# A Hadamard transform of weights in two exact single-pass halves instead of one full-precision product

## The chip, the cores and the metric

The kernel runs on one core of one Trainium2 chip. The metric is the time of one execution on the device in microseconds (us). A core has five engines that run their own instruction queues in order: PE (TensorE, matrix products), DVE (VectorE), ACT (ScalarE), POOL (GpSimd) and SP (SyncE, which only issues DMAs here). "PEld" is PE's loading of the stationary operand, which overlaps with its products.

## The reference, cut to what matters

The input `x` is 8 sequences of 512 tokens of 512 features, all float32. Each token is layer-normalized. One branch is linear attention (three projections, `elu + 1`, a running sum over tokens, an output projection), the other a gated feed-forward layer whose weights stand behind Walsh-Hadamard transforms (`fwht`); their product is added to `x`:

```
x = fwht(xn * SU_ug) / SCALE
x_up   = x @ W_up.T   * (Wscale_ug[:INTER] * SCALE)
x_gate = x @ W_gate.T * (Wscale_ug[INTER:] * SCALE)
x = fwht(silu(x_gate) * x_up * SU_dp) / SCALE
g = silu(x @ W_down.T * (Wscale_dp * SCALE))
out = x0 + attention(xn) * g
```

A transform of a product's input is the same as a transform of its weights, so the kernel transforms the three weight matrices (512 x 2048 each) once, on the chip, and then multiplies by those. A transform over 512 features splits into a 128-point one across the partitions, which is a product with the 128x128 matrix of plus and minus ones (`had`), and two rounds of butterflies (sum and difference) between the four blocks of 128. Over 2048 features there are four such rounds.

## The kernel before, in words

**Work and stages.** The eight sequences go in four pairs (p = 0 to 3). For a pair, all large products (q, k, v, out, gate, up, down) are done by a fast scheme that makes a 2x2 block product from seven factor products (places P1 to P7, in the order P1, P2, P7, P3, P4, P5, P6 of a tile `[128, 2, 7, 128]`); the weights' seven factors are encoded by four DVE instructions per block (`encode_weights`, lines 310 to 315). In the first pair the weights are also prepared: read, transformed, encoded and written to DRAM, from which the later pairs stream them ready-made. So everything that the change touches lies in the first pair, before about 360 us of the profiled span.

**The gate and up weights** (`folded_w`, line 926) are 16 blocks (gate 0 to 7, up 0 to 7). For each there are three steps: `butterflies` (four DVE instructions of 512 elements per partition, lines 937 to 940, into a fresh tile of the pool `t8`), `fold` (two matmuls with `had`, line 946, each followed by two ACT scalings of 256 columns by the signs `SU_ug`, line 952, from PSUM back into the weights' tile), and `encode`. The first product of the block's group waits for the scalings and the encoded places.

**The down weights** are four blocks of 16 tiles (o = 0 to 3): `butterflies_down` makes scale and four rounds on DVE (lines 979 and 984) in the buffer `rd`, then `fold_down` (line 993) does four matmuls with `had` (line 998), each with four ACT scalings of 128 columns (line 1004), and the block goes to DRAM (`wd_f`, line 1010). `chain_down` strings the four blocks together.

**Order.** The program is traced in an order set by an agenda: `at(n, fn)` puts a step n places ahead, one place being about one factor product, and `advance` runs them (lines 430 to 443). A list scheduler then orders each engine's queue by priority and readiness; the matmuls of the folds are held in the order of the program (`keep_in_program_order`). What comes out is a fixed queue per engine, and an engine waits at the head of its queue. PSUM banks of the folds are the tag `t`, which has two buffers, so that a fold's matmul also waits until the scalings of the fold two before it have read their bank. The groups' banks are `px` (3 buffers), `py` (1) and `pz` (2); DVE and ACT read them out (lines 465 to 476).

**Other work named later.** POOL encodes the attention's context `co` (`encode_tokens`, lines 303 to 307), the output weights `w_o` (lines 312 to 315) and the hidden activations `ho` (lines 800 to 802: products of gate and up; then lines 304 to 307). ACT makes `neg_k` and `neg_q` (lines 710 and 711) for `elu`, and DVE takes those up at line 712.

Of the kernel before, what the change touches and what calls it, by code (L numbers as in the profile page):

```python
# [7 lines left out]

F32 = mybir.dt.float32
AF = mybir.ActivationFunctionType  # L10
ALU = mybir.AluOpType
PSUM = bass.MemoryType.PSUM
# [5 lines left out]
P1, P2, P7, P3, P4, P5, P6 = range(7)  # L18
# [3 lines left out]
def kernel(  # L22
# [27 lines left out]
    nc = tc.nc  # L50
    P = 128
# [4 lines left out]
    NF = FF // P  # L56
# [6 lines left out]
    const = ctx.enter_context(tc.tile_pool(name="const", bufs=1))  # L63
# [4 lines left out]
    t8 = ctx.enter_context(tc.tile_pool(name="t8", bufs=6))  # L68
# [5 lines left out]
    @contextmanager  # L74
    def background(behind=150):

        at = tc.cur_priority
        tc.cur_priority = at + behind
        yield
        tc.cur_priority = at  # L80
# [20 lines left out]

    cols_sb = const.tile([P, cols.shape[1]], F32, tag="cols", name="cols_sb")
    offs = {}
    at = 0
# [9 lines left out]

    bo_r = const.tile([P, D], F32, tag="bo_r", name="bo_r")
    ident = const.tile([P, P], F32, tag="ident", name="ident")
    had = const.tile([P, P], F32, tag="had", name="had")
    ones = const.tile([P, 1], F32, tag="ones", name="ones")
    su_ug = const.tile([P, KD], F32, tag="su_ug", name="su_ug")
    su_dp = const.tile([P, NF], F32, tag="su_dp", name="su_dp")  # L120
# [13 lines left out]
    def layernorm(b, xt, parts=1):  # L134
        n = NT // parts
        for i in range(0, NT, n):
# [6 lines left out]
            nc.vector.tensor_scalar(rstd, mv[:, :, 1], EPS, None, ALU.add)  # L143
            nc.scalar.activation(rstd, rstd, AF.Sqrt)
            nc.vector.reciprocal(rstd, rstd)
# [6 lines left out]
    def first_layernorms(xs):  # L152
# [8 lines left out]
        def pinned(ins):  # L161
            tc.keep_in_program_order(ins)

        for i in range(2 * NT + 1):
            if i < 2 * NT:
# [4 lines left out]
                pinned(nc.vector.tensor_scalar(r, mv[:, i, 1:2], EPS, None, ALU.add))  # L170
                nc.scalar.activation(r, r, AF.Sqrt)
            if i:
# [10 lines left out]
    def normalized(b):  # L183
# [246 lines left out]
    def at(place, fn):  # L430
        agenda.append((now[0] + place, now[1], fn))
        now[1] += 1
# [17 lines left out]
    def group(name, ws, rhs, dst, then, bias=(None, None), time=1.7):  # L450
# [14 lines left out]
        def snapshot(what, i):  # L465
# [5 lines left out]
            else:  # L471
                nc.scalar.activation(s, p, AF.Identity, bias=b)
            return s
# [218 lines left out]
    def attention(p, xo, co, get_w):  # L692
        def project(m, g, then):
# [4 lines left out]
            def whole(px):  # L698
                nc.scalar.activation(r[:, 0, 1], px, AF.Identity, bias=b[0])
                then(r)  # L700
# [219 lines left out]
    def butterfly(eng, dst, src, h):  # L920
# [2 lines left out]
        eng.tensor_tensor(d[:, :, 0], s[:, :, 0], s[:, :, 1], ALU.add)  # L923
        eng.tensor_tensor(d[:, :, 1], s[:, :, 0], s[:, :, 1], ALU.subtract)

    def folded_w(name, src, f, room=None):

        w = raw_w(f"{name}_{f}", src, 0, 2, 1, f * P, NG * P, room)
        places = (slice(P1, P7 + 1, 2), slice(P2, P4 + 1, 3))
        rs = []  # L930

        def butterflies():
            t = t8.tile([P, 2, 2, 2, 2, P], F32, tag="t", name=f"r_{name}_{f}")
            r2, r = t[:, 0], t[:, 1]
            rs.append(r)
            a, b = (w[:, :, place, :] for place in places)
            nc.vector.tensor_tensor(r2[:, 0], a, b, ALU.add)
            nc.vector.tensor_tensor(r2[:, 1], a, b, ALU.subtract)
            nc.vector.tensor_tensor(r[:, :, 0], r2[:, :, 0], r2[:, :, 1], ALU.add)
            nc.vector.tensor_tensor(r[:, :, 1], r2[:, :, 0], r2[:, :, 1], ALU.subtract)  # L940

        def fold():
            for b in range(2):
                p = ps.tile([P, 2, 2, P], F32, tag="t", name=f"pw_{name}_{f}_{b}")
                tc.keep_in_program_order(
                    nc.tensor.matmul(
                        p.rearrange("p j a e -> p (j a e)"), had,
                        rs[0][:, b].rearrange("p j a e -> p (j a e)"), start=True, stop=True,
                    )
                )  # L950
                for j in range(2):
                    nc.scalar.activation(
                        w[:, j, places[b], :], p[:, j], AF.Copy, scale=su_ug[:, 2 * b + j : 2 * b + j + 1]
                    )
        def encode():
            encode_weights(nc.vector, w)
            folded[name, f] = w
            if f >= NU:
                with background():
                    inner_w(name, f - NU, folded[name, f - NU], w)  # L960

        return w, [(5, butterflies), (7, fold), (9, encode)]

    folded = {}
    wd_f = dram.tile([FF, D], F32, tag="wd_f", name="wd_f")
# [3 lines left out]
    def load_down(o):  # L969
        at(14, lambda: loaded.append(o))  # L970
        nc.sync.dma_start(rs[:, o % 2], wdown_t[:, o * P : (o + 1) * P].rearrange("(c p) e -> p c e", p=P))
# [18 lines left out]
                later(1.2, half, i, dst, src, h)  # L990
        later(0.0, then)

    def fold_down(o, a, then):

        r = rs[:, o % 2]
        p = ps.tile([P, 4, P], F32, tag="t", name=f"pwd_{o}_{a}")
        tc.keep_in_program_order(
            nc.tensor.matmul(
                p.rearrange("p c e -> p (c e)"), had,
                r[:, 4 * a : 4 * a + 4].rearrange("p c e -> p (c e)"), start=True, stop=True,  # L1000
            )
        )
        for c in range(4):
            nc.scalar.activation(
                r[:, 4 * a + c], p[:, c], AF.Copy, scale=su_dp[:, 4 * a + c : 4 * a + c + 1]
            )
        if a + 1 < NF // 4:
            at(2, lambda: fold_down(o, a + 1, then))
            return
        nc.sync.dma_start(wd_f[:, o * P : (o + 1) * P].rearrange("(c p) e -> p c e", p=P), r)  # L1010
        then()
# [49 lines left out]
    def weights_ahead(u):  # L1061

        def begin(m, src, f):
            t = t8.tile([P, 2, 7, P], F32, tag="t", name=f"w_{m}_{f}")
            _, steps = folded_w(m, src, f, t)
            place = 10
            for _, step in steps:
                at(place, step)
                place += 7

        at_ = 2
        for m, src in (("gate", wgate_t), ("up", wup_t)):
            for f in (u, u + NU):
                at(at_, lambda m=m, src=src, f=f: begin(m, src, f))
                at_ += 12
# [64 lines left out]
    src = ident  # L1140
    for i in range(7):
        dst = had if i % 2 == 0 else had2
        s = src.rearrange("p (a t h) -> p a t h", t=2, h=1 << i)
# [3 lines left out]
        src = dst  # L1147
# [14 lines left out]
    rs = rd[:, : 3 * NF * P].rearrange("p (i c e) -> p i c e", i=3, e=P)  # L1162
# [8 lines left out]
    def chain_down(o):  # L1171
        if o not in loaded:
            at(2, lambda: chain_down(o))
            return

        def folded_block():
            if o + 2 < KD:
                at(8, lambda: load_down(o + 2))
            if o + 1 == KD:
                at(8, first_half_down)  # L1180

        def then():
            at(10, lambda: fold_down(o, 0, folded_block))
            if o + 1 < KD:
                at(4, lambda: chain_down(o + 1))

        butterflies_down(o, then)
# [116 lines left out]
```

## Time and profile before

| what | value |
|---|---|
| median of 3 runs | 1555.47 us (1553.84 to 1557.9) |
| span of the profiled execution, first to last instruction | 1552.4 us |
| what the median has beyond that span | 3.1 us |
| PE idle inside the span (span less busy) | 28.6 us |

The profile gives only the span of its own execution; its whole time is taken to be the span and the 3.1 us around it.

The same engine times by stretch, from the table of windows (busy us of each engine):

| stretch, us | PE | DVE | ACT | POOL |
|---|---|---|---|---|
| 0 to 69 | 60.3 of 69 | 60.9 | 30.3 | 6.9 |
| 69 to 138 | 63.4 of 69 | 64.9 | 34.5 | 33.2 |
| 138 to 430 | 283.5 of 292 | 215.7 | 81.4 | 71.9 |
| 430 to 1552 | 1116.6 of 1122 | 660.8 | 272.7 | 324.7 |

To read such tables: an engine that is busy all the time need not be the one that sets the end, since work can be queued on it that nobody needs yet. The chain of waits says which engine the end was waiting for at each moment. "Busy" of DVE and POOL also counts the time in which an instruction has started but stands still. PE had its full granted clock (0.998 on average).

### The profile page before, as it was taken

The page shows a single profiled execution, that of the slowest core. Times are in us where ns is not written, and L with a number is a line of the kernel's source. Part 1 is how long each engine was busy: PE and PEld are TensorE (multiplying, and loading weights), DVE is VectorE, ACT ScalarE, POOL GpSimd, SP SyncE. Part 2 cuts the span into 40 slices and gives each one's busy share as a digit, 9 for nine tenths or more (in the row PEclk, how much of TensorE's full clock was granted, in tenths as well). Part 3 has the DMA queues.
Part 4 walks back from the last instruction along what each step waited for, and adds up shares of the span by engine and source line. Part 5 has one row for each costly group of instructions (what it writes and reads, how often), then busy time and mean ns, then how long its engine had stood idle before and what let it go on. Part 6 is the DMA issues. An engine that isn't in the chain of part 4 may idle for free.

```text
span 1552.4 us, 15693 instructions
## 1 busy us (share of the span) xinstructions
PE 1523.8 (98%) x5924; PEld 1121.3 (72%) x5924; DVE 1002.4 (65%) x1423; ACT 418.9 (27%) x664; POOL 436.7 (28%) x236
## 2 busy tenths in 40 slices
PE   7989999999999999999999999999999999999998
PEld 3436446746874588888884488888886478888887
DVE  7989787378867665516767674715675575533673
ACT  4452341141125411112114431111213431111211
POOL 1232233004320261205511144302621126210631
PEclk9999999999999999999999999999999999999999
DMA  8345877687985244354576344335574233535462
GB/s 276 98 141 176 258 250 240 214 276 261 267 283 162 90 154 160 95 166 164 166 265 235 93 143 149 114 119 186 175 245 155 87 112 102 191 100 174 164 258 81
DMA packets 197692, 273.31 MB, mean 176 GB/s; under 512 B 56816, under 2 KB 155120, under 8 KB 193392
## 3 DMA queue, kind: packets, MB, share of 16 engines
q1 hardware_dynamic: 197472, 272.27, 54.0%
q8 instruction: 47, 0.77, 0.2%
q14 instruction: 29, 0.24, 0.0%
q10 hardware_dynamic: 144, 0.03, 0.0%
HBM read 196.25 MB, written 76.02 MB: 175 GB/s over the span
## 4 chain that ended last, share of the span: by engine, by line
PE 90%; DVE 6%; DMA 1%; ACT 1%; issue 1%; SPq 0%; POOL 0%; POOLq 0%; DVEq 0%; ACTq 0%
PE px_gu L638 20%; PE px_dn L536 13%; PE pz_gu L638 10%; PE pz_dn L536 6%; PE py_gu L638 5%; PE px_k L460 4%; PE py_dn L536 4%; PE px_o L536 3%; PE px_v L460 3%; PE px_q L460 3%; PE px_up L460 2%; PE pz_o L536 2%; PE pz_k L460 2%; PE pz_v L460 2%; PE pz_q L460 2%; PE px_gate L460 1%
## 5 line engine op out<-in xcount | busy, mean ns | idle before, releaser
L638 PE MATMUL px_gu<-xo,w_gu 128*128 128x256 f32 x1456 | 347.7, 380 | 1.4 <-DVE sb_gu L648 1.4
L638 PEld LDWEIGHTS px_gu<-xo,w_gu 128*128 128x128 f32 x1456 | 275.7, 190 | 45.9 <-issue 5.0
L536 PE MATMUL px_dn<-w_down,ho 128*128 128x256 f32 x1024 | 228.7, 379 | 0.0
L536 PEld LDWEIGHTS px_dn<-w_down,ho 128*128 128x128 f32 x1024 | 194.6, 190 | 28.6 <-issue 2.4
L638 PE MATMUL pz_gu<-xo,w_gu 128*128 128x256 f32 x728 | 187.7, 380 | 1.1 <-DVE u L476 1.1
L838 POOL TENSOR_TENSOR u<-u,v 128x1024 f32<-128x1024 f32 x26 | 61.0, 2367 | 365.9 <-DVE u L676 347.4
L638 PEld LDWEIGHTS pz_gu<-xo,w_gu 128*128 128x128 f32 x728 | 137.5, 190 | 22.3 <-DVE u L476 1.5
L536 PE MATMUL pz_dn<-w_down,ho 128*128 128x256 f32 x496 | 112.5, 379 | 1.7 <-DVE u L476 1.7
L536 PEld LDWEIGHTS pz_dn<-w_down,ho 128*128 128x128 f32 x496 | 93.7, 190 | 16.4 <-DVE u L476 2.1
L638 PE MATMUL py_gu<-xo,w_gu 128*128 128x256 f32 x364 | 93.4, 379 | 0.0
L304 POOL TENSOR_TENSOR co<-co 128x512 f32<-128x512 f32 x8 | 14.6, 1829 | 266.3 <-DVE co L737 266.3
L883 POOL TENSOR_TENSOR s<-s,d 128x512 f32<-128x512 f32 x30 | 40.0, 1333 | 165.4 <-ACT d L882 165.4
L638 PEld LDWEIGHTS py_gu<-xo,w_gu 128*128 128x128 f32 x364 | 69.2, 190 | 9.4
L842 POOL TENSOR_TENSOR v<-v,r 128x1024 f32<-128x1024 f32 x26 | 60.9, 2361 | 26.9 <-DVE r L676 26.9
L460 PE MATMUL px_k<-xo,w_k 128*128 128x512 f32 x128 | 61.8, 606 | 0.0
L460 PE MATMUL px_v<-xo,w_v 128*128 128x512 f32 x128 | 60.6, 594 | 0.0
L460 PE MATMUL px_q<-xo,w_q 128*128 128x512 f32 x128 | 60.3, 592 | 0.0
L828 ACT ACTIVATE a<-a,cols_sb 128x512 f32<-128x512 f32 x26 | 18.7, 721 | 149.5 <-DVE a L676 147.8
L882 ACT ACTIVATE d<-d 128x512 f32<-128x512 f32 x31 | 19.5, 630 | 144.4 <-DVE d L551 124.7
L536 PE MATMUL px_o<-w_o,co 128*128 128x256 f32 x256 | 58.2, 379 | 0.0
L828 ACT ACTIVATE u<-u,cols_sb 128x512 f32<-128x512 f32 x52 | 36.9, 720 | 78.2 <-DVE u L676 75.0
L536 PE MATMUL py_dn<-w_down,ho 128*128 128x256 f32 x256 | 57.9, 379 | 0.0
(269 smaller groups left out, 2417.4 us busy)
## 6 DMA issues: line engine op xcount, KB each, us to landing
w_gu<-d_gu SPq DMA_DIRECT2D x91, 896.0 KB, 4.5
w_down<-d_down SPq DMA_DIRECT2D x56, 512.0 KB, 3.8
d_s<-o SPq DMA_DIRECT2D x8, 1024.0 KB, 5.7
d_d<-dn SPq DMA_DIRECT2D x8, 1024.0 KB, 7.7
d<-d_d SPq DMA_DIRECT2D x8, 1024.0 KB, 6.3
s<-d_s SPq DMA_DIRECT2D x8, 1024.0 KB, 8.1
y<-in_x_dram SPq DMA_DIRECT2D x8, 1024.0 KB, 6.4
out_dram<-y SPq DMA_DIRECT2D x15, 512.0 KB, 3.2
```

The source lines that it names most:

```text
L304: eng.tensor_tensor(o[..., P5, :], o[..., P7, :], o[..., P1, :], ALU.subtract)
L460: nc.tensor.matmul(p.rearrange("p a t -> p (a t)") if len(r.shape) == 2 else p, ws[k][:, i, :], r, start=(first and k == 0), stop=(k == n ...
L536: nc.tensor.matmul(p[:, c], t[:, (2 * g + c) * P : (2 * g + c + 1) * P], ws[i](k), start=(first and k == 0 and c == cs[0]), stop=(k == n - ...
L638: nc.tensor.matmul(p[:, lane], w[:, lane, i, :], x[:, i, :], start=(first and lane == 0), stop=True, skip_group_check=True,)
L828: nc.scalar.activation(g[:, m], g[:, m], AF.Silu, scale=col("w_gate", u + m * NU + a * NG))
L838: nc.gpsimd.tensor_tensor(r[:, m], ru1[:, m], rv[:, m], ALU.add)
L842: nc.gpsimd.tensor_tensor(rv[:, m], rv[:, m], rr[:, m], ALU.add)
L882: nc.scalar.activation(d, d, AF.Silu)
L883: (nc.vector if final and (a, s) == (1, 0) else nc.gpsimd).tensor_tensor(r, r, d, ALU.mult)
```

## The change

The matrix `had` and the operand of every fold become `float32r`, a 4-byte type that the change means to have multiplied in a single pass with a shorter mantissa. So that nothing is lost, each operand is split into two parts that are exact in that type: ACT copies it into a `float32r` tile (the high part), POOL subtracts the copy from the original (the low part), and PE does two matmuls, high then low, into the same PSUM bank. The new helpers are `two_parts` and `by_had`. The gate and up butterflies no longer write a fresh tile but overwrite free places of the loaded weights' tile; the tile of `t8` now holds the two parts. Of the six DVE instructions, two have 512 elements and four have 256. A new step `parts_down` makes the parts of one quarter of a down block, two places apart, and the fold follows six places after its parts. The `fold` of gate and up stands nine places after the butterflies (seven before), and in `weights_ahead` steps are nine places apart (seven before).

```diff
-    had = const.tile([P, P], F32, tag="had", name="had")
+    had = const.tile([P, P], F32R, tag="had", name="had")
...
+    def two_parts(t, r, view):
+        high, low = (view(t[:, i]) for i in range(2))
+        nc.scalar.copy(high, r)
+        nc.gpsimd.tensor_tensor(low, r, view(t[:, 0].bitcast(F32)), ALU.subtract)
+        return t
+
+    def by_had(p, parts):
+        for i in range(2):
+            tc.keep_in_program_order(
+                nc.tensor.matmul(p, had, parts[:, i], start=(i == 0), stop=(i == 1))
+            )
...
         def butterflies():
-            t = t8.tile([P, 2, 2, 2, 2, P], F32, tag="t", name=f"r_{name}_{f}")
-            r2, r = t[:, 0], t[:, 1]
-            rs.append(r)
             a, b = (w[:, :, place, :] for place in places)
-            nc.vector.tensor_tensor(r2[:, 0], a, b, ALU.add)
-            nc.vector.tensor_tensor(r2[:, 1], a, b, ALU.subtract)
-            nc.vector.tensor_tensor(r[:, :, 0], r2[:, :, 0], r2[:, :, 1], ALU.add)
-            nc.vector.tensor_tensor(r[:, :, 1], r2[:, :, 0], r2[:, :, 1], ALU.subtract)
+            diff = w[:, :, P5 : P6 + 1, :]
+            nc.vector.tensor_tensor(diff, a, b, ALU.subtract)
+            nc.vector.tensor_tensor(a, a, b, ALU.add)
+            for r, src in zip(whole, (a, diff)):
+                nc.vector.tensor_tensor(r[:, 1], src[:, 0], src[:, 1], ALU.subtract)
+                nc.vector.tensor_tensor(r[:, 0], src[:, 0], src[:, 1], ALU.add)
+            t = t8.tile([P, 2, 2, 2 * 2 * P], F32R, tag="t", name=f"r_{name}_{f}")
+            for b in range(2):
+                parts.append(two_parts(t[:, b], whole[b], lambda x: x.rearrange("p (j a e) -> p j a e", j=2, a=2)))
...
-        return w, [(5, butterflies), (7, fold), (9, encode)]
+        return w, [(5, butterflies), (9, fold), (9, encode)]
...
+    def parts_down(o, a, then):
+        r = rs[:, o % 2, 4 * a : 4 * a + 4].rearrange("p c e -> p (c e)")
+        t = t8.tile([P, 2, 4 * P], F32R, tag="t", name=f"rd_{o}_{a}")
+        parts = two_parts(t, r, lambda x: x)
+        at(6, lambda: fold_down(o, a, parts, then))
+        if a + 1 < NF // 4:
+            at(2, lambda: parts_down(o, a + 1, then))
...
-            at(10, lambda: fold_down(o, 0, folded_block))
+            at(6, lambda: parts_down(o, 0, folded_block))
```

More of the change, by code (lines that the diff above doesn't have):

```diff
@@ L9 @@
 F32 = mybir.dt.float32
+F32R = mybir.dt.float32r
 AF = mybir.ActivationFunctionType
@@ L929, in folded_w @@
         places = (slice(P1, P7 + 1, 2), slice(P2, P4 + 1, 3))
-        rs = []
+        rows = w.rearrange("p j s e -> p (j s) e")
+        whole = (
+            rows[:, 0:4].rearrange("p (a j) e -> p j a e", j=2),
+            rows[:, 4:14].rearrange("p (j x) e -> p j x e", j=2)[:, :, 1:3],
+        )
+        parts = []
         def butterflies():
-            t = t8.tile([P, 2, 2, 2, 2, P], F32, tag="t", name=f"r_{name}_{f}")
-            r2, r = t[:, 0], t[:, 1]
-            rs.append(r)
             a, b = (w[:, :, place, :] for place in places)
-            nc.vector.tensor_tensor(r2[:, 0], a, b, ALU.add)
-            nc.vector.tensor_tensor(r2[:, 1], a, b, ALU.subtract)
-            nc.vector.tensor_tensor(r[:, :, 0], r2[:, :, 0], r2[:, :, 1], ALU.add)
-            nc.vector.tensor_tensor(r[:, :, 1], r2[:, :, 0], r2[:, :, 1], ALU.subtract)
+            diff = w[:, :, P5 : P6 + 1, :]
[7 more added lines that the diff above has]
+                parts.append(two_parts(t[:, b], whole[b], lambda x: x.rearrange("p (j a e) -> p j a e", j=2, a=2)))
         def fold():
@@ L944, in fold @@
                 p = ps.tile([P, 2, 2, P], F32, tag="t", name=f"pw_{name}_{f}_{b}")
[L945 to L950, printed above, removed]
+                by_had(p.rearrange("p j a e -> p (j a e)"), parts[b])
                 for j in range(2):
@@ L991, in butterflies_down, with fold_down @@
         later(0.0, then)
-    def fold_down(o, a, then):
+    def parts_down(o, a, then):
[5 more added lines that the diff above has]
+            at(2, lambda: parts_down(o, a + 1, then))
+    def fold_down(o, a, parts, then):
         r = rs[:, o % 2]
         p = ps.tile([P, 4, P], F32, tag="t", name=f"pwd_{o}_{a}")
[L997 to L1002, printed above, removed]
+        by_had(p.rearrange("p c e -> p (c e)"), parts)
         for c in range(4):
@@ L1007, in fold_down @@
         if a + 1 < NF // 4:
-            at(2, lambda: fold_down(o, a + 1, then))
             return
@@ L1068, in begin @@
                 at(place, step)
-                place += 7
+                place += 9
         at_ = 2
```

## The prediction, as it went on record

> **What bounds it now.** I read the shares first. PE is busy nearly the whole span and DVE two thirds of it, so an edit counts if it takes work from PE, or where PE is not what is waited for.
>
> ```profile
> span 1552.4 us, 15693 instructions
> PE 1523.8 (98%) x5924; PEld 1121.3 (72%) x5924; DVE 1002.4 (65%) x1423; ACT 418.9 (27%) x664; POOL 436.7 (28%) x236
> PE 90%; DVE 6%; DMA 1%; ACT 1%; issue 1%; SPq 0%; POOL 0%; POOLq 0%; DVEq 0%; ACTq 0%
> ```
>
> The third line is the chain of waits: 6% of it, about 93 us, hangs on DVE. Where? The chain in order of time, between 69 and 138 us, is almost all DVE; I show its largest pieces and the place where ACT takes over.
>
> ```profile
> 69.05 2.27 DVE rd L984 x2
> ...
> 75.48 1.76 DVE r_gate L940
> 77.23 3.34 DVE rd L979 x2
> ...
> 98.07 5.93 DVE k L729 x4
> ...
> 105.81 1.47 ACT w_gate L952 x4
> 107.28 0.94 ACT neg_q L710
> ```
>
> So there are three stretches: up to 69 us nothing changes; from 69 to 138 DVE sets the pace; after that PE does to the end. From 138 us the table of windows gives PE 283.5 of 292 us to 430, then 1116.6 of 1122.
>
> The third view is the groups by shape, for what the folds cost, and the timeline for their cadence.
>
> ```profile
> L998 PE MATMUL pwd<-rd,had 128*128 128x512 f32 x32 | 16.5, 605 | 5.6 <-ACT w_gate L952 3.7 <-ACT rd L1004 1.9
> L946 PE MATMUL pw_gate<-r_gate,had 128*128 128x512 f32 x32 | 15.6, 611 | 2.2 <-DVE r_gate L940 2.2
> L946 PE MATMUL pw_up<-r_up,had 128*128 128x512 f32 x32 | 15.2, 592 | 0.0
> ```
>
> There are 96 records for 48 matmuls, two each. In the timeline a dense row of four records of 128x512 starts every 1.72 us (85.56, 87.27, 88.99), so a record costs 0.43 us, a fold matmul 0.86, and all 48 cost 41.2 us.
>
> **What the change takes and adds.** Matmuls: 48 become 96 of float32r. No row shows one. Above it stands the 0.43 us of a float32 record of the same size, below it the 0.19 us of a load of 128 columns of weights, which each matmul has. The shortest dense cadence of a record is that of 128x256 (16 of px_dn in 3.45 us, 0.216 each). I take 0.215, near the lower end, since the floor of 0.19 is the nearest row to it. Then a fold costs 0.43 in place of 0.86 and PE loses 48 x 0.43 = 20.6 us; at the upper bound it loses nothing, at the lower 22.9.
>
> POOL: 48 subtractions of 128x512. Rows of this size (line 883) take 1.26 us alone and up to 1.64; line 304 shows a median of 2.13 beside a busy DVE. ACT: 48 copies; a copy of that size takes 0.585 (line 646), and lines 710 and 711 take 1.06 per 1024 from SBUF. I take 0.6. DVE: four instructions of 0.60 (start to start) become two of 0.60 and four of 0.34 (lines 312 to 315), 0.16 more per block.
>
> The cost that the counts don't show is what POOL does to DVE. Here is POOL, then DVE, at 67 to 80 us:
>
> ```profile
> 66.86 2.14 POOL L304 TENSOR_TENSOR co<-co 128x512 f32<-128x512 f32 x1 [60.93 <-DVE co L737]
> 69.07 5.93 POOL L305 TENSOR_TENSOR co<-co 128x512 f32<-128x512 f32 x1
> 74.97 1.72 POOL L307 TENSOR_TENSOR co<-co 128x512 f32<-128x512 f32 x1
> 76.65 1.71 POOL L306 TENSOR_TENSOR co<-co 128x512 f32<-128x512 f32 x1
> ```
>
> ```profile
> 73.79 0.68 DVE L476 TENSOR_TENSOR k<-sb_k,pz_k 128x512 f32<-128x512 f32 x1
> 74.39 1.17 DVE L939 TENSOR_TENSOR r_gate<-r_gate 128x512 f32<-128x512 f32 x1
> 75.48 1.76 DVE L940 TENSOR_TENSOR r_gate<-r_gate 128x512 f32<-128x512 f32 x1
> 77.16 3.42 DVE L979 TENSOR_TENSOR rd<-rd 128x1024 f32<-128x1024 f32 x2
> ```
>
> POOL's second instruction stands for 5.9 us until DVE reaches one that reads PSUM; then the two alternate, and DVE's 0.68 becomes 1.17 and 1.76, its 2.35 becomes 3.42. That is 0.49 + 1.08 + 1.07 = 2.64 us of DVE for four POOL instructions, 0.66 each; at 112 to 127 us eight of them cost DVE 4.3, 0.54 each. I take 0.6 per added subtraction where DVE has no slack; the bounds are 0 and POOL's whole 1.26.
>
> [...]
>
> **Stretch 69 to 138, on DVE.** Twelve fold matmuls lie there (down blocks 0 and 1, gate 0 and 4). Their 12 x 0.43 us go from PE, which is not waited for, so they bring nothing. DVE gets 12 x 0.6 = 7.2 for contention and, with up 0 and 4, whose butterflies lie at its end, 4 x 0.16 = 0.6. And a new wait: in the changed program's queues the first subtraction, of down block 0, stands on POOL behind the four `co` instructions above, which end at 78.4; so the first fold ends near 80 (PE reached it at 70.3). On ACT the scaling of that fold now stands ahead of `neg_k`, for which DVE's line 712 waits: scaling 1.1, three copies 1.8, then the first two results of `neg_k` 3.2, to about 86, where DVE arrives at 83.4 (80.5 before, plus what it was delayed). I charge 2.5; nothing if POOL gets in earlier, 5 if later. Sum: +10.3.
>
> **From 138 on, on PE.** The other 36 matmuls give 36 x 0.43 = 15.5 us. Against it stand PE's waits for parts that come late, because POOL's queue is in order and holds work that waits for PE itself:
> - up 0: its six DVE instructions, two copies and two subtractions follow one another directly, 2.6 + 1.2 + 2.7, and PE arrives about 2.5 us early.
> - down block 3. POOL's queue reads: part 1, `ho` line 304, `ho` line 802 (old lines), part 2, `ho`, gate 1 first half, `ho`, gate 1 second half, part 3. The `ho` at line 802 waits for DVE's read of the last bank of up 0. From there it is 2.4 + 6 x 1.26 = 10 us to the end of part 3, plus 1 for DVE, and PE has only its own 5 us between that bank and the last fold. That is 6 us. ACT stands alike: three copies (1.9) are queued between the two halves of a scaling whose PSUM bank the next fold needs, 2.5 more. Bounds 2 and 13.
> - up 4, up 1 and gate 2 are folded directly ahead of their group's first product (5 us ahead before, gate 2 none), which then waits for the scalings, 0.95 each, and for the snapshots: 3.
> Sum 14; the bounds are 4 and 22. After 340 us no fold is left, and the queues are the old ones but for a few swapped rows, which I cost at nothing; each such swap is a product or two of 0.43.
>
> **The sum.** 10.3 - 15.5 + 14 = +8.8 us on the execution profiled, span 1552.4 and 3.1 around it, 1555.5, which is the median of the runs: 1564.
>
> **Rivals.**
> *The parts are ready in time* (faster). POOL is busy only 33 of 69 and 72 of 292 us, so capacity is there, and the new distances (six places, 5.2 us, for a copy and a subtraction of 1.9) look enough. The waits would have to fall to about 4 and DVE's charge to the 0.8 of its own instructions or 3: 3 - 15.5 + 4 = -8.5, down to -15.5 with none. It decides from where delay on DVE and waits on PE together stay below 15.5. Centre 1544. Against it: POOL's order above.
> *It cancels:* delays of 12 to 19 us leave 1551 to 1560, nothing to measure.
> *DVE pays the whole price:* 12 x 1.26 = 15 in the middle, and each POOL instruction 1.7, as beside a busy DVE, in the queue ahead of down block 3 (8 x 0.4 = 3 more), and up 1, 4 and gate 2 each a further 1: 1564 + 8 + 3 + 3 = 1578.
> *The float32r pass is no shorter* than a float32 record: the 15.5 are missing, 1580. Only the two bounds speak for it.
>
> **Chances.** Forecast 0.42 (1556 to 1572); parts ready 0.28 (1540 to 1550); cancelling 0.10; whole price 0.16; no shorter pass 0.04. About 0.3%, 4.7 us, is what a measurement can tell from no change. The forecast's own lower tail, 0.07, is within it: faster 0.28, same 0.17, slower 0.55. The range takes in the whole price and the longer pass with some room, 1585, and below most of the first rival, 1539, leaving out about 1 in 10 on each side or less.
>
> **What would show it.** In the changed profile: matmul records of line 938, x96 or x192, with a cadence near 0.215; the first fold at 80, not 70; POOL's subtractions above 1.3 and DVE rows of line 979's kind stretched; idle time of PE ahead of line 938, released by POOL, of some 15 us in all, most of it before down block 3's last fold; and the first product of gate 1 at about 204 us, where it was at 187.9 (10.3 plus 12 of the 14, less 12 of the 36 matmuls, 5.2). I am wrong if the chain between 69 and 138 is PE, or if PE's idle time from 69 to 340 us (271 less 260.2 busy) stays near the old 10.8 us.

## The result, and the profile after

The changed kernel takes 1605.5 us (median of 4 runs, 1604.0 to 1606.5) against 1554.7 (4 runs): a ratio of 1.033, 95% interval 1.031 to 1.0342. It is slower, as forecast, but by 51 us and not by 9. (Here a whole execution is 1.8 us longer than its span, 1605.5 against 1603.7, and not the 3.1 that were taken.)

The head of its page, whose lines answer to the first three of the prediction:

```profile
span 1603.7 us, 15835 instructions
PE 1526.9 (95%) x5924; PEld 1126.2 (70%) x5924; DVE 1044.4 (65%) x1455; ACT 440.2 (27%) x710; POOL 509.1 (32%) x284
PE 79%; DVE 8%; POOL 4%; issue 3%; DMA 3%; ACT 1%; SPq 0%; POOLq 0%; DVEq 0%; ACTq 0%
```

PE is idle for 76.8 us of the span (28.6 before), and POOL and "issue" have joined the chain of waits. PE's busy time has risen by 3.1 us, although the folds now cost less: four float32r passes in a row take 0.93 us, so a pass is 0.232 and a fold of two 0.465 in place of 0.859, 18.9 us for all 48. Busy time that grows while work shrinks has two sources. A pass that stands alone counts as some 0.5 us (0.50 at 124.13 us), more than it takes in a row; and PE ran slower, as the table of windows says. The same stretch, before and then after (columns: length, then busy time and instructions of PE, PEld, DVE, ACT and POOL, the granted clock, DMA share, GB/s):

```profile
69.00:340.00 271.00, 260.18 (x766) 145.21 (x765) 210.70 (x288) 96.75 (x202) 70.26 (x35) 0.99 0.69 217
```

```profile
69.00:340.00 271.00, 226.38 (x678) 132.14 (x677) 220.33 (x272) 100.75 (x213) 130.99 (x75) 0.94 0.58 181
```

PE idles 44.6 us of these 271 (10.8 before), the granted clock falls from 0.99 to 0.94, and POOL is busy 61 us more. DVE, for all its 220 us, got 16 instructions fewer done.

What PE waited for after the change (engine, line, what it waited for, total us, times, longest):

```profile
PE pwd L938 <- POOL rd L931: 14.7, 7, 6.8
PE px_dn L537 <- DMA w_down<-d_down: 8.9, 2, 7.5
...
PE pw_up L938 <- ACT rd L1026: 6.5, 1, 6.5
PE px_gate L461 <- DVE w_gate L314: 6.0, 3, 4.6
PE pz_dn L537 <- DVE u L477: 4.0, 1, 4.0
PE pw_up L938 <- POOL r_up L931: 3.5, 6, 0.9
PE pw_up L938 <- ACT r_up L930: 3.4, 2, 1.8
PE pw_gate L938 <- POOL r_gate L931: 2.8, 3, 1.3
```

Only the lines with POOL and the copies of L930 are direct waits for parts, 24 us in these rows. And each long wait has a tail. PE's timeline at the first fold (start, us, what; the wait ahead of a row in brackets):

```profile
71.38 0.79 PE L938 MATMUL pwd<-rd,had 128*128 128x512 f32 x1
78.98 0.79 PE L938 MATMUL pwd<-rd,had 128*128 128x512 f32 x1 [6.81 <-POOL rd L931]
79.57 3.62 PE L461 MATMUL px_v<-xo,w_v 128*128 128x512 f32 x4
```

After the wait of 6.81 us the four records of `px_v` take 3.62 us, where four take 1.88 before it. The clock was at half from 77 us on for 6.83 us (granted clock 0.50 between 77.27 and 84.10). Up to 500 us the trace has six such spells, of 6.83, 3.41, 13.65, 3.41, 6.83 and 10.24 us: 44 us at half pace. PE was busy in 31 of them, so some 15.5 us of its work were lost. The kernel before has one, of 3.41.

To see where the time is lost, I compare the start of the same product in both traces (its first row in the timeline):

| product | before | after | later by |
|---|---|---|---|
| first `py` of the output projection | 135.3 | 146.4 | 11.1 |
| `py` of gate 1 | 189.5 | 219.0 | 29.5 |
| first `py` of the first down product | 264.6 | 303.7 | 39.1 |
| the same, second half | 422.5 | 462.6 | 40.1 |
| `py` of the second pair's first k | 458.8 | 510.2 | 51.4 |

From there to the end nothing more is lost. The last 11 us are far behind the last fold. SP's queue at that place, before and then after:

```profile
415.46 3.06 SPq L339 DMA_DIRECT2D w_down<-d_down  x2
...
419.56 0.65 SPq L916 DMA_DIRECT2D y<-in_x_dram  x1
421.01 2.05 SPq L339 DMA_DIRECT2D w_down<-d_down  x2
431.58 0.38 SPq L916 DMA_DIRECT2D y<-in_x_dram  x1
433.10 0.32 SPq L339 DMA_DIRECT2D w_down<-d_down  x1
```

```profile
462.76 1.09 SPq L340 DMA_DIRECT2D w_down<-d_down  x1
...
465.27 13.27 SPq L917 DMA_DIRECT2D y<-in_x_dram  x2
478.59 1.73 SPq L340 DMA_DIRECT2D w_down<-d_down  x3
```

Before, the second load of `y`, whose buffer comes free late, stands behind two loads of `w_down`. After, both loads of `y` stand ahead of three; 13 us pass until the queue reaches those, PE waits 7.5 us for `w_down`, and 10.24 us of half clock follow.

### The profile page after: what moved, and what is told of

It is laid out like the page before. It is cut to its first block, busy times and chain, and to the rows that moved or that the text cites. A ratio compares the mean times of both kernels' runs of the same rounds, so it can differ in the third digit from the quotient of the medians.

```text
span 1603.7 us, 15835 instructions
## 1 busy us (share of the span) xinstructions
PE 1526.9 (95%) x5924; PEld 1126.2 (70%) x5924; DVE 1044.4 (65%) x1455; ACT 440.2 (27%) x710; POOL 509.1 (32%) x284
## 4 chain that ended last, share of the span: by engine, by line
PE 79%; DVE 8%; POOL 4%; issue 3%; DMA 3%; ACT 1%; SPq 0%; POOLq 0%; DVEq 0%; ACTq 0%
PE px_gu L639 19%; PE px_dn L537 12%; PE pz_gu L639 10%; PE pz_dn L537 5%; PE py_gu L639 5%; PE px_k L461 4%; PE px_v L461 3%; PE py_dn L537 3%; PE px_o L537 3%; PE px_q L461 3%; PE pz_k L461 2%; PE pz_o L537 2%; PE pz_q L461 1%; PE pz_v L461 1%; PE px_up L461 1%
## 5 line engine op out<-in xcount | busy, mean ns | idle before, releaser
L537 PEld LDWEIGHTS pz_dn<-w_down,ho 128*128 128x128 f32 x496 | 95.5, 193 | 18.6 <-DVE u L477 4.4
```

The costliest lines, as they stand in the source:

```text
L537: nc.tensor.matmul(p[:, c], t[:, (2 * g + c) * P : (2 * g + c + 1) * P], ws[i](k), start=(first and k == 0 and c == cs[0]), stop=(k == n - ...
```

## The experiments

Three theories stood at the start. **A:** parts come late, PE waits, and the half clock doubles the price. **B:** the longer distances and the queues that they reorder cost the time. **C:** POOL's subtractions cost by slowing DVE (and POOL's own later work), whether or not somebody waits for them. Ratios are to the kernel before, with 95% intervals; differences between experiments are of medians. Single executions of one kernel spread by 1 to 9 us here (11 in `e15_fill_gate`), so places in single traces are trusted to some 4 us. The kernel before, run beside each group of experiments, had medians from 1551.8 to 1554.7, so a difference between experiments of two groups is good to some 3 us.

### The gain alone, and the distances alone

`e6_short_alone`: DVE's last butterfly writes the rounded part itself; one pass, old distances.

```diff
-            for r, src in zip(whole, (a, diff)):
+            t = t8.tile([P, 2, 2, 2 * P], F32R, tag="t", name=f"r_{name}_{f}")
+            for b, src in enumerate((a, diff)):
+                r = t[:, b].rearrange("p j (a e) -> p j a e", a=2)
                 nc.vector.tensor_tensor(r[:, 1], src[:, 0], src[:, 1], ALU.subtract)
                 nc.vector.tensor_tensor(r[:, 0], src[:, 0], src[:, 1], ALU.add)
...
-        for h, dst, src in ((8, r2, r), (4, r, r2), (2, r2, r), (1, r, r2)):
+        for h, dst, src in ((8, r2, r), (4, r, r2), (2, r2, r), (1, t, r2)):
```

> The gain alone: one float32r pass for each fold at the old distances; DVE writes the rounded value itself, so no copies on ACT, no subtractions on POOL, and the butterflies run in the weights' room. (The low parts are left out of the result.) If PE's time from 138 us on is the end's time, as the forecast has it, 36 x (0.859 - 0.232) = 22.6 us go: 1532, and two passes alone would be worth 14 (1541). If the fold time is covered anyway, 1550 or more.

1554.5 us, ratio 1.001 (0.9996 to 1.0024). Thirty us less of PE work bring nothing. Up to the second half of the first down product its trace leads by 12 us (410.6 against 422.5); at the second pair's k the lead is 0.6, since its SP queue, too, has both `y` ahead of three `w_down` (7.4 us of wait, 10.24 of half clock).

`e7_butterflies`: the kernel before with the butterflies of the change and nothing else.

```diff
-            nc.vector.tensor_tensor(r2[:, 0], a, b, ALU.add)
-            nc.vector.tensor_tensor(r2[:, 1], a, b, ALU.subtract)
...
+            nc.vector.tensor_tensor(diff, a, b, ALU.subtract)
+            nc.vector.tensor_tensor(a, a, b, ALU.add)
...
+            rs.extend(whole)
```

> The kernel before with the butterflies in the weights' room alone: six DVE instructions in place of four, no parts, one full float32 matmul a fold, old distances. By the forecast 0.16 us more of DVE for a block: 1555 to 1558. If every shift in this part makes SP's queue put both y ahead of three loads of w_down, as with the longer distances, 12 more: about 1567.

1554.2, 1.0004 (0.9992 to 1.0016). That part of the change is free, and it leaves SP's order as it was.

`e11_two_alone`: as `e6`, the pass done twice.

```diff
-        for i in range(1):
+        for i in range(2):
             tc.keep_in_program_order(
-                nc.tensor.matmul(p, had, parts[:, i], start=(i == 0), stop=True)
+                nc.tensor.matmul(p, had, parts[:, 0], start=(i == 0), stop=(i == 1))
```

> Two float32r passes a fold and nothing else of the split: as the run with one short pass alone, with the pass done twice on the same rounded part and the scale halved (the low part itself is left out). 48 x 0.232 = 11.1 us more PE work than with one pass (1554.5). If PE sets the end, 1564 to 1566; if PE's waits there take it up, 1555 to 1558. Either way no gain over the kernel before, though the folds take 18.9 us less.

1562.4, 1.0055 (1.0038 to 1.0072). So **the two passes would have gained nothing even if the parts had cost nothing.** By the second half of the first down product (421.9 us, 422.5 before) the 18.9 us saved are gone. From the windows between 69 and 420 us, PE is idle 24.2 us in place of 14.2, and it is busy for 18.2 us at half clock in place of 3.4 (granted clock 0.96 to 0.97 in the windows from 69 to 380 us, 0.99 to 1.00 before), which loses 7.4 us more: together nearly the saving. The new waits are for DVE (18.6 us in place of 8.6); the two longest of these rows were 0.7 and 1.7 us before:

```profile
PE px_gate L461 <- DVE w_gate L314: 7.1, 2, 6.1
...
PE pz_dn L537 <- DVE u L477: 4.2, 1, 4.2
```

The order at `y` then makes it slower. But PE's time is not worthless there: `e6`, with another 11.1 us less, is 11.3 us ahead of `e11` at that place. Why the first 18.9 us vanished and the next 11 counted isn't shown.

`e3_places`: the kernel before with the new distances.

```diff
-        return w, [(5, butterflies), (7, fold), (9, encode)]
+        return w, [(5, butterflies), (9, fold), (9, encode)]
-                place += 7
+                place += 9
-            at(10, lambda: fold_down(o, 0, folded_block))
+            at(12, lambda: fold_down(o, 0, folded_block))
```

> The kernel before with the changed kernel's distances alone: fold 9 places behind the butterflies in place of 7, steps of 9 in the background, the first fold of a down block at 12 in place of 10. No parts, full float32 matmuls. Theory A: within 5 us of the kernel before, 1550 to 1560. Theory B: most of the loss is here, 1580 to 1600.

1578.6, 1.0174 (1.0156 to 1.0191). Theory B holds for 24.6 us: 13.6 of them by the second half of the first down product (with one wait of 6.2 us in `px_gate` for encoded places of `w_gate`, which come later when the fold does), and 11 after it, at `y`.

`e10_old_places`: the changed kernel with the old distances.

```diff
-        return w, [(5, butterflies), (9, fold), (9, encode)]
+        return w, [(5, butterflies), (7, fold), (9, encode)]
-                place += 9
+                place += 7
-            at(6, lambda: parts_down(o, 0, folded_block))
+            at(4, lambda: parts_down(o, 0, folded_block))
```

> The changed kernel with the old distances (fold 7 places behind the butterflies, background steps of 7, the first fold of a down block at 10). Alone, the longer distances cost 24.6 us, 13.6 of them before the second half of the first down product. If the two causes add up, these 13.6 come back and the order at y stays: 1592. If the longer distances are what keeps the parts from being later still, PE's waits for POOL grow by as much and the time is 1600 to 1615.

1596.2, 1.027 (1.0252 to 1.0288): 9.2 of the 13.6 come back, and the order at `y` stays. The causes add up but for some 4 us.

### The order at `y`

`e4_y_pool`: in the first pair the loads of `y` are issued by POOL.

```diff
-        nc.sync.dma_start(y, x[2 * p + s].rearrange("(n p) d -> p n d", p=P))
+        (nc.gpsimd if p == 0 else nc.sync).dma_start(y, x[2 * p + s].rearrange("(n p) d -> p n d", p=P))
```

> The changed kernel with the two loads of y for the first pair of batches issued from POOL's queue; on SP's queue they stood for 11.8 us ahead of three loads of w_down. If that order is the cause of the 7.5 us in which PE waits for w_down at 485 us, the wait goes and with it the half clock behind it (10.2 us long, 5 us of work lost): 1605 to about 1593. If w_down is late for another reason (full DMA queues), nothing changes: 1605.

1600.7, 1.0308 (1.0288 to 1.0327). The wait and the half clock go, and the stretch from the second half of the first down product to the second pair's k takes 39.1 us (47.5 in the change, 36.3 before). But only 4.8 us reach the end: 4 are lost right behind it, where PE waits 2.2 us for ACT in the first k and gets 3.41 us of half clock.

`e8_short_y`: the same edit on `e6`.

> The kernel with one short pass alone (1554.5: 30 us less of PE work for no gain), with the two early loads of y on POOL's queue. If the wait for w_down and the half clock behind it ate the gain, 7.4 us of wait and about 5 of half clock go: 1542. If the gain was never on the path, 1554.

1549.1, 0.9974 (0.9962 to 0.9986): 5.4 better than `e6`, not 12.

`e17_short_order`: `e6` with the loads of `y` still on SP's queue, 40 places of priority later.

```diff
+            with background(40):
+                nc.sync.dma_start(y, src)
```

> One short pass alone (1554.5; the low parts are left out), with the early loads of y on SP's queue but 40 places of priority later, so that two loads of w_down stand ahead of them. The stretch from the second half of the first down product to the second pair's k took 47.6 us in that run and 36.2 in the kernel before. If the order of these five loads is all of it, 11 us go: 1543. If it is the order in POOL and ACT as well, as with y on POOL, 1549.

1548.3, 0.9973 (0.9962 to 0.9983). The stretch takes 37.3 us as against 47.6, so the order of five loads is what it cost; in this execution 5.7 us of that had been lost earlier. By medians it is worth 6.3 us.

### POOL's subtractions

`e1_high_only`: the changed kernel without the subtractions and the low pass.

```diff
-        nc.gpsimd.tensor_tensor(low, r, view(t[:, 0].bitcast(F32)), ALU.subtract)
...
-        for i in range(2):
+        for i in range(1):
```

> The changed kernel without the low parts: no subtractions on POOL, one float32r pass a fold; ACT's copies and all distances stay. (The low bits of the transformed weights are left out of the result.) Theory A, that PE stands waiting for POOL's subtractions and the clock gate then halves its pace: 11 us of passes (48 x 0.232), about 21 us of PE waits released by POOL and some 10 us of half clock go, 1605 to about 1563; PE waits on ACT (banks of tag t) stay. Theory B, that the longer distances and the new order of queues cost the time: only the 11 us go, 1594.

1564.5, 1.0079 (1.0064 to 1.0095), close to theory A's 1563; but the 24.6 us of `e3_places` belong to neither, so the agreement proves nothing. The head of its page:

```profile
PE 1507.6 (97%) x5876; PEld 1116.0 (71%) x5876; DVE 1011.9 (65%) x1455; ACT 439.6 (28%) x710; POOL 433.3 (28%) x236
```

DVE has the same 1455 instructions as the changed kernel and is busy 1011.9 us, there 1044.4. So 48 subtractions on POOL cost DVE 32.5 us, 0.68 each, while POOL spent 75.8 on them, 1.58 each.

`e2_low_dve`: the subtraction on DVE.

```diff
-        nc.gpsimd.tensor_tensor(low, r, view(t[:, 0].bitcast(F32)), ALU.subtract)
+        nc.vector.tensor_tensor(low, r, view(t[:, 0].bitcast(F32)), ALU.subtract)
```

> The changed kernel with the low part's subtraction on DVE in place of POOL, nothing else. Theory A (POOL's queue makes the parts late): the waits that POOL releases shrink, half the half-clock time goes, DVE takes 48 x 0.62 = 30 us more of which 12 x 0.62 = 7 lie where DVE sets the pace; about 1585. Theory B (distances and order): the same as the change, 1600 to 1610. [...]

1585.6, 1.0215 (1.0198 to 1.0232), 20 us faster than the change. DVE's busy time is the same in both (1046.9 and 1044.4): giving the work to POOL relieved DVE of nothing, and the 20 us are not DVE's time but what POOL did late.

`e12_copy_dve`: the copies on DVE, the subtractions on POOL.

```diff
-        nc.scalar.copy(high, r)
+        nc.vector.tensor_copy(high, r)
```

> The changed kernel with the copies of the high part on DVE in place of ACT. If copies in ACT's queue, ahead of the scalings that empty the banks of tag t, cost the 6.5 us wait at 200 us, the 4.3 us of waits on copies and some 5 us of half clock behind them, about 15 go, less 7 that DVE loses in the stretch it sets: 1597. If DVE's time is dearer than ACT's order, 1605 or more.

1610.3, 1.0363 (1.0345 to 1.0381). Taking the copies out of ACT's queue gained nothing: the 6.5 us wait for a bank is no longer among the long ones, but PE waits 11 us for copies on DVE instead. What they cost in ACT's queue isn't shown by this.

`e14_detached`: POOL subtracts, but both passes read the high part.

```diff
-                nc.tensor.matmul(p, had, parts[:, i], start=(i == 0), stop=(i == 1))
+                nc.tensor.matmul(p, had, parts[:, 0], start=(i == 0), stop=(i == 1))
```

> The changed kernel in which POOL still makes every subtraction, but both passes of a fold read the high part (scale halved), so that no matmul waits for POOL; the low parts are left out of the result. If lateness of the parts is what costs (PE's 21 us of waits released by POOL and some 8 of half clock behind them), the time falls to about 1576. If what costs is POOL's traffic beside DVE and the delay of its other work (ho, co), the time stays near 1600.

1599.6, 1.0306 (1.029 to 1.0321). With none of PE's 21 us of waits for POOL, only 6 us are gained. That does not yet settle theory A, since someone else still waited for POOL (ACT's waits, 60 to 420 us, here and then in the changed kernel):

```profile
ACT rd L1026 <- POOL rd L931: 14.9, 5, 10.2
```

```profile
ACT rd L1026 <- PE pwd L938: 23.1, 9, 11.1
```

The scaling overwrites the very weights that the subtraction reads, so ACT stands until POOL has read them. In the changed kernel it stands for PE, whose second pass has itself waited for POOL. So `e14` moved the lateness of the low parts from PE to ACT and did not take it away.

`e18_beside`: POOL's 48 instructions read the high part twice instead; now nothing waits for them but their buffers.

```diff
-        nc.gpsimd.tensor_tensor(low, r, view(t[:, 0].bitcast(F32)), ALU.subtract)
+        again = view(t[:, 0].bitcast(F32))
+        nc.gpsimd.tensor_tensor(low, again, again, ALU.subtract)
```

> As the run with nobody waiting in PE for POOL's subtractions (1599.6), but each reads the high part twice in place of the weights: there ACT's scaling, which overwrites those weights, still had to wait for POOL (14.9 us). Now nothing waits for POOL's 48 instructions but their buffers and POOL's own later work; the low parts are left out. If lateness is what costs, by way of ACT, about 1575, as 1564.5 of the run with high parts alone and 8 for the second pass give 1572. If POOL's traffic beside DVE (36 us more of DVE's busy time) and its late ho and co cost, 1590 to 1600.

1589.4, 1.0229 (1.0205 to 1.0253): nearest to theory C, but both have a share. `e1` plus the 7.9 us of a second pass (`e11` less `e6`) is 1572. From there 17 us are due to POOL's instructions running at all (theory C), and the 16 from `e18` to the change to somebody's waiting for them (theory A): 10 of these remain when only PE is freed (`e14`). `e2`, where DVE does the same work and POOL has none of it, is 13 above 1572.

### The clock

`e5_fill`: 24 passes of `had` by itself ahead of the first fold of the changed kernel.

```diff
+        if (o, a) == (0, 0):
+            for _ in range(24):
+                tc.keep_in_program_order(
+                    nc.tensor.matmul(p, had, had.unsqueeze(1).to_broadcast([P, 4, P]), start=True, stop=True)
+                )
```

> The changed kernel with 24 extra float32r passes (5.6 us, the plus-minus-one matrix by itself, overwritten afterwards) ahead of the first fold, where PE stood for 6.8 us. If the slow products behind that wait come from the clock gate, the 6.8 us at half clock from 77 us on go, the products of px_v there take 1.9 and not 3.6 for four, the first product of gate 1 comes about 3 us earlier and the time is 1602; work added makes the kernel faster. [...]

1604.9, 1.0332 (1.0317 to 1.0348). PE's timeline:

```profile
71.22 6.02 PE L1027 MATMUL pwd<-had 128*128 128x512 f32 x24
...
78.92 0.50 PE L938 MATMUL pwd<-rd,had 128*128 128x512 f32 x1 [1.45 <-POOL rd L931]
79.26 1.88 PE L461 MATMUL px_v<-xo,w_v 128*128 128x512 f32 x4
...
84.77 0.79 PE L938 MATMUL pwd<-rd,had 128*128 128x512 f32 x1 [3.40 <-POOL rd L931]
```

The records of `px_v` are back at 1.88 for four: their slowness was the clock's, not that of DVE or of memory. But the time stays, since PE reached the next fold sooner only to wait 3.40 us for its low part: here POOL sets the pace. Nor did half clock go: a spell of 6.83 us now begins at 83.5 us (behind that wait two records of `px_q` take 1.91 us), and up to 500 us there are 44 us of it in all, as in the change (mean granted clock 0.986 in both). So the run doesn't tell what half clock costs.

`e15_fill_gate` and `e19_fill_order`: the same filling ahead of gate 5's first product, on `e8` and on `e17`, where no part of POOL's follows.

```diff
+            if name == f"gate_0_{NU + 1}":
+                for _ in range(24):
+                    nc.tensor.matmul(
+                        px.rearrange("p a t -> p (a t)"), had, had.unsqueeze(1).to_broadcast([P, 4, P]),
+                        start=True, stop=True, skip_group_check=True,
+                    )
             product(px, P1, True)
```

> The run with one short pass and y on POOL's queue (1549.1) with 24 extra passes (5.6 us, overwritten) ahead of the first product of gate 5, where PE stands 6.2 us for DVE and then has 6.8 us of half clock. Here no late part of POOL stands behind it. If the clock gate costs the end 3.4 us, 1546: faster with work added. If DVE is what the next products wait for anyway, 1549 to 1551.

1550.6, 0.9981 (0.9966 to 0.9997), with executions from 1542.9 to 1554.1, 1.5 us above `e8` by medians. The same with `y` on SP's queue:

> The run with one short pass and y 40 places of priority later (1548.3) with 24 extra passes (5.6 us, overwritten) ahead of the first product of gate 5, where PE stands 6.2 us. With y on POOL's queue the same filling let the second gate's py product come 4.5 us later and the third up's 2.8 us earlier, but the times spread from 1543 to 1554. If half clock costs the end 3.4 us, 1545; if not, 1548 to 1549.

1544.9, 0.9948 (0.9928 to 0.9968), against 1548.3 without the filling. `e17` and then `e19` at that gate:

```profile
207.37 3.75 PE L461 MATMUL px_gate<-xo,w_gate 128*128 128x512 f32 x4 [6.21 <-DVE w_gate L314]
...
211.78 3.82 PE L461 MATMUL pz_gate<-xo,w_gate 128*128 128x512 f32 x8
```

```profile
206.25 1.95 PE L461 MATMUL px_gate<-xo,w_gate 128*128 128x512 f32 x4 [0.86 <-DVE w_gate L314]
...
208.50 3.60 PE L461 MATMUL pz_gate<-xo,w_gate 128*128 128x512 f32 x8
```

At that gate the 5.6 us of useless work take the half clock away (granted clock between 180 and 220 us: 1.00, in `e17` 0.91), and the last of these products comes 3.3 us earlier. Whether the end gains is less sure: by medians 3.4 us here, but the two intervals touch, the two ran in different groups, and on `e8` the same filling gained nothing. The spells in the traces of before and after, up to 500 us, are all multiples of 3.41 us. Which wait brings one isn't shown: the kernel before has a spell of 3.41 us at 306 us behind a single wait of 2.24 us, and a wait of 3.72 us at 103 us, in the same trace, brought no half clock.

### Where it might have paid

`e13_mixed`: `e8` with full float32 folds for down blocks 0 and 1 and gate 0 and 4.

```diff
-            t = t8.tile([P, 2, 2, 2 * P], F32R, tag="t", name=f"r_{name}_{f}")
+            t = t8.tile([P, 2, 2, 2 * P], F32 if f in (0, NU) and name == "gate" else F32R, tag="t", name=f"r_{name}_{f}")
...
-        t = t8.tile([P, NF, P], F32R, tag="t", name=f"rd_{o}")
+        t = t8.tile([P, NF, P], F32 if o < 2 else F32R, tag="t", name=f"rd_{o}")
```

> One short pass a fold with y on POOL's queue (1549.1), but full float32 matmuls for the folds of down blocks 0 and 1 and of gate 0 and 4, which lie where DVE sets the pace. (The low parts of the other folds are left out.) There PE's time is not waited for and work only keeps the clock up: 3 us of half clock go, 1546, if those folds stay off the path; 1549 to 1554 if they are on it.

1553.5, 1.0 (0.9989 to 1.001), 4.4 slower than `e8`. The first `py` of the output projection comes at 138.2 us against 130.8: 7.4 us for 12 folds longer by 0.627, that is 7.5. They lie on the path there, where the forecast had DVE alone set the pace; 4.4 us of it reach the end.

`e16_late_only`: the exact split for gate and up 2, 3, 6 and 7 alone, full folds elsewhere, old distances, `y` behind two loads of `w_down`. In `butterflies`, against `e7`:

```diff
-            rs.extend(whole)
+            if f % NU < 2:
+                rs.extend(whole)
+                return
+            t = t8.tile([P, 2, 2, 2 * 2 * P], F32R, tag="t", name=f"r_{name}_{f}")
+            for b in range(2):
+                rs.append(two_parts(t[:, b], whole[b], lambda x: x.rearrange("p (j a e) -> p j a e", j=2, a=2)))
```

> The change where there is time for it: two parts for gate and up blocks 2, 3 and 6, 7 alone (16 folds, 16 x 0.39 = 6.3 us), full float32 folds for the rest and the down blocks, old distances, butterflies in the weights' room, and the early loads of y put behind two loads of w_down by 40 places of priority. If parts there are ready in time and the order holds, 1549; if their copies and subtractions make the same waits, 1554 to 1560.

1559.4, 1.0048 (1.0031 to 1.0064). Sixteen folds, each 0.39 us shorter, do not pay for their parts there either.

The fastest kernel tried is `e19_fill_order`, but like every kernel here that beats the one before it drops the low parts, so it isn't the same arithmetic. No exact split was faster than the kernel before.

## Why the prediction was wrong

The 51 us, step by step from the kernel before (1554), as medians:

| step | us | from |
|---|---|---|
| one short pass for each fold, with SP's new order at `y` | 0 | `e6` |
| second pass | +8 | `e11` less `e6` |
| ACT's copies and the longer distances | +10 | `e1` less `e6` |
| POOL's instructions run beside the rest | +17 | `e18` less 1572 |
| low parts late, ACT waits for them | +10 | `e14` less `e18` |
| low parts late, PE waits as well | +6 | the change less `e14` |

1572 is the time of `e1` and a measured difference and was not run. Each step begins where the one before it ends, so the sum is 51 by itself; the steps depend on their order, and each is good to some 3 us (by ratios the last two are 12 and 3).

**The stretch from 69 to 138 us: +10.3 forecast, 11.1 measured** at the first product behind it. The agreement is in good part luck. The new wait came as described: the first fold ended near 80 us (78.98 and one pass) and `neg_k` at 86.3. But "on DVE" was wrong. The chain of waits of the changed kernel has 27 us in POOL's instructions there and 8 in DVE's (0 and 60 before); three of its pieces:

```profile
97.74 2.66 POOL r_gate L931
...
103.80 2.19 POOL r_gate L931
...
121.87 2.21 POOL rd L931
```

PE waits 10.7 us for POOL's parts of the down blocks in that stretch and 5.5 for `w_gate`. The price of a subtraction to DVE, 0.6 taken, was 0.68 over all 48. That is near the 0.66 and 0.54 of the two places in the trace of before that it was taken from, and far from POOL's whole 1.26, the upper bound. And that PE's shorter folds are worth nothing there is not so in `e13`.

**"From 138 on, on PE ... the other 36 matmuls give 15.5 us."** This is the step that failed most. From the first `py` of the output projection to the second half of the first down product the forecast had -1.5 us (14 less 15.5), and 29.0 came. The pass was right (0.232 for 0.215), the worth was not: in `e11`, with the parts for nothing, 18.9 us of saving left 0.6. PE was busy 97% of that stretch and still not alone in setting the pace, since DVE's sums, encodings and butterflies follow right behind; in `e11` time taken from PE turned into waits for DVE, and these into half clock. (Why the further 11 us of `e6` did count stays open.) The sign named for it, gate 1's first product "at about 204" (the prediction's own sum gives 205), came at 217.3. A full engine with idle time of only 8.5 us looks like the bound, but the chain of waits says only what was last, not how close the next one stood.

**The price of POOL to DVE was charged to 12 subtractions, not to 48.** The other 36, by the measured 0.68, are 24 us of DVE's time that I took for slack by the same reasoning. `e18` shows 17 us for all 48 with nobody waiting. How much of that is DVE's slowing and how much POOL's late `ho`, `co` and `w_o` is open; the 13 us of `e2`, with as much DVE time and no work of POOL's late, suggest that DVE's part is the larger.

**"Sum 14; the bounds are 4 and 22"** for PE's waits. Behind the first `py` of the output projection PE waits 21 us ahead of line 938, for parts and banks together, more than the forecast's 14 but inside its bounds. PE's idle time between 69 and 340 is 44.6 us, where the signs named the old 10.8 and "some 15". By `e18` the lateness of the low parts costs 16 us in all, and freeing PE alone would not have saved it (`e14`).

**The clock had no term at all.** PE was busy for 31 us at half pace, some 15.5 us of its work. The trace of before had the evidence, one spell of 3.41 us behind a wait of 2.24. It isn't a cause by itself: it makes a wait dearer where PE is what is waited for. How much of it reaches the end no run here settles (`e5` kept as much of it, and `e15` and `e19` differ).

**"After 340 us no fold is left ... a few swapped rows, which I cost at nothing."** One of those swaps cost 11 us in place, 5 to 6 by the medians of `e4`, `e8` and `e17`. It was in the changed program's queues to be seen: a load that waits for a buffer, moved ahead of loads that were ready. What in the scheduler turns it isn't settled; distances alone turn it (`e3`) and so does the one short pass (`e6`); butterflies alone don't (`e7`).

**The rivals.** "The parts are ready in time" would have given 1544: it falls twice, since free parts don't gain (`e11`) and the exact split where it seemed to have time doesn't (`e16`). "DVE pays the whole price", 1578, came nearer, and its reason is half right: POOL's instruction at 1.58 us is near the 1.7 that it took, DVE's price at 0.68 is not its 1.26. "No shorter pass", 1580, falls by the 0.232.

## What to carry to other kernels

Before costing a saving at its full length, take the saved work out by itself (or ask how far behind the next engine stands): at 97% busy, the first 18.9 us freed here went into waits and half clock. Charge an added instruction on POOL to DVE wherever DVE is at all busy (0.68 us for each of 48 here), and ask who overwrites what it reads as well as who reads what it writes: freeing the reader alone left the overwriter waiting (`e14`). Look through every queue for a waiting load that has moved ahead of ready ones, also far behind the edit.

## What the runs showed of the hardware

Half clock came in spells of 3.41 us and multiples (3.41 to 13.65 in the traces of before and after), behind single waits of PE from 1.87 us up (`e5`, at 404 us) or two or three shorter ones within some 5 us (1.64 and 0.86 in the change, ending at 246.7 and 248.1 us). Not each wait brought it: one of 3.75 us (`e2`, at 277 us) did not, while every longer one in these traces did, the start of the kernel aside. Filling one such wait with useless passes took the half clock behind it away (four records in 1.95 us in `e19`, in place of 3.75 in `e17`). POOL's 128x512 subtraction from SBUF took 1.58 us and lengthened DVE's time by 0.68, about what DVE needs to do it itself (0.73 more of DVE's time for each in `e2`). A float32r pass of 128x512 takes 0.232 us against 0.43 for one record of float32, of which a product has two.
